# Moving two layers' seam: layer 2's first scores before layer 1's last down products, and a root taken on GpSimd

## The chip, the cores and the metric

The kernel runs on one core of a Trainium2 chip. A core has TensorE for matrix products (PE in the profile, its weight loads PEld), VectorE (DVE), ScalarE (ACT), GpSimd (POOL) and SyncE (SP), which here only starts transfers. Each engine works through its own queue of instructions in order, and waits at the head of the queue on semaphores of the others. The metric is the time of one execution on the device, in microseconds; lower is better.

## The reference

The whole is a stack of four layers over x of shape (4, 256, 256), that is 1024 tokens of width 256. Each layer adds a gated attention and a gated feed-forward, each over a layer norm of x:

```
x = x + tanh(g_xattn[n]) * attention_n(layernorm(x), ctx)
x = x + tanh(g_ffn[n])   * ffn_n(layernorm(x))

def layernorm(x):  (x - mean) / sqrt(var + 1e-5)

# layer 1's ffn: ternary weights
h = gelu(x @ w1_q.T + b1)            # 256 -> 1024
out = h @ w2_q.T + b2                # 1024 -> 256

# layer 2's attention: 16 heads of 16, 64 keys
scores = (q @ Wq.T) . k / 4, causal
out = softmax(scores) . v @ Wout.T

# layer 2's ffn: whole numbers of 8 bits
y = round(x / x_scale) @ round(w / w_scale).T * x_scale * w_scale + bias
```

The change lies at the seam between layer 1's feed-forward and layer 2's attention.

## The kernel before

The 1024 tokens are 8 tiles of 128 (t = 0 to 7), each held in SBUF as x[t]; four tiles make a group of 512 (g = 0, 1). The program is written as a list of steps (attention and feed-forward of the four layers). The order on each engine's queue is settled when the program is built, by a scheduler that takes instructions by their dependencies and by the order in which the code names them. `behind(later, sooner)` adds an order without a wait; `side_by_side` raises the priority of products that belong together. Tiles come from pools with a fixed number of buffers: four banks of PSUM under the tag mm, two double banks under wide, so a product may also wait until an older result has been copied out.

**Layer 1's feed-forward** (`ffn1`). `up(g)` makes the hidden values of a group in three bf16 terms, `down(g, i, terms)` multiplies them with the ternary w2 for one tile: 24 matmuls in one PSUM bank (L1920), then y = product + bias (L1928) and x[t] = gate * y + x[t] (`gated_add`, L517). The hidden values lie in the upper part of the large buffer `big`, where layer 3's last experts are to be loaded, so `load_experts3(EARLY3, E3)` and the load that follows `used("L1_w2")` wait for the last products.

Around the last four down products, `ffn1` already prepares layer 2: `keys_values` makes the keys and the values in steps (L1000, L1007, L1016, L171 and L169), `layernorm(0)` normalises group 0, `transposed` turns it (L461, copies L169 and L171), `head_queries` multiplies it with Wq (L476) and scales it in ScalarE (L1034). In the code the order is: down 0, normalise, down 1, down 2, down 3, transpose, queries.

**`layernorm`** (L425 to L452): for each tile the statistics (L430, L433) on VectorE; then for the group's four variances at once, in a tile of 128x4, the square root of var + eps on ScalarE (L435) and its reciprocal on VectorE (L438); then x - mean times that, tile by tile, on VectorE (L449), or, for layers where `scalar` is set, on ScalarE (L446) with a shift made on VectorE (L442).

**Layer 2's attention** (`attention23`). `scores(t)` makes one tile's scores: for even t a causal mask is put in first (L1065), then four products (L1075), the maximum over the keys (L1090), the difference in two halves (L1092) on VectorE, the exponential (L1101) on ScalarE. `weights` sums (L490), takes the reciprocal (L491) on VectorE and multiplies on GpSimd (L492). `attend(t)` transposes the weights (L506), copies them in ScalarE (L507), multiplies with the values (L1109), copies (L1118) and multiplies with Wout (L1121); `gated_add` (L517) then adds to x[t]. `in_flight` names these in stages: scores of tile i, the addition of tile i-3, the weights of tile i-1, the attend of tile i-2. In each of its rounds it takes one step of a generator `beside`: here `queries(1)`, which normalises, turns and multiplies group 1, together with the keys and values for layer 3 and, near the end, `rounded(0)`, the first part of layer 2's feed-forward.

[...] The profile shows a load (ACT_TABLE_LOAD, 1.28 us) where the queue goes from the gelu to the root, from the root to the exponential, and back to the root for layer 2's feed-forward.

Of the kernel before, what the change touches and what calls it, by code (L numbers as in the profile page):

```python
# [30 lines left out]
F32 = mybir.dt.float32  # L31
# [66 lines left out]
def tile_flamingo(ctx: ExitStack, tc: tile.TileContext, a: dict, out: bass.AP):  # L98
# [39 lines left out]
    def small(shape, name, bufs=3, dtype=F32):  # L138
        return sb.tile(shape, dtype, tag=name, name=name, bufs=bufs)

    def behind(later, sooner):

        tc.add_manual_dep(
            later.ins,
            sooner.ins.name,
            mybir.DependencyInfo(mybir.DependencyClass.NoSync, mybir.DependencyReason.DATA),
            reason="not sooner",
        )

    def side_by_side(products):  # L150

        last = None
        for product in products:
            with tc.high_priority(AT_ONCE) if last else nullcontext():
                made = product()
            if last:
                behind(made, last)
            last = made
        return last
# [26 lines left out]
    nc.gpsimd.memset(ones, 1.0)  # L186
    eps = const.tile([P, 1], F32, tag="eps", name="eps")
    nc.gpsimd.memset(eps, EPS)
    root = small([P, 1], "root", 1)
    nc.scalar.activation(root, eps, AF.Sqrt)  # L190

# [119 lines left out]
    def used(name):  # L311

        del loaded[name]
        at[1] += 1
        issue()
# [106 lines left out]
            nc.sync.dma_start(out=tiled(sums, layer)[:, t, :], in_=x[t])  # L422


    def layernorm(g, scalar=False, after=()):  # L425

        mv = small([P, TPG, 2], "mv")
        for i in range(TPG):
            st = small([P, 6], "st")
            made = nc.vector.bn_stats(st, x[g * TPG + i])  # L430
            if after:
                behind(made, after[0])
            nc.vector.bn_aggr(mv[:, i, :], st)  # L433
        rstd = small([P, TPG], "rstd")
        made = nc.scalar.activation(rstd, mv[:, :, 1], AF.Sqrt, bias=eps)  # L435
        if after:
            behind(made, after[1])
        nc.vector.reciprocal(rstd, rstd)  # L438
        xn = []
        if scalar:  # L440
            shift = small([P, TPG], "shift")
            nc.vector.scalar_tensor_tensor(shift, mv[:, :, 0], -1.0, rstd, ALU.mult, ALU.mult)  # L442
        for i in range(TPG):
            n = sb.tile([P, D], F32, tag="xn", name="xn", bufs=AHEAD + 2)
            if scalar:
                nc.scalar.activation(n, x[g * TPG + i], AF.Identity, bias=shift[:, i : i + 1], scale=rstd[:, i : i + 1])  # L446
                xn.append(n)
                continue
            kept["normal"] = nc.vector.tensor_scalar(  # L449
                n, x[g * TPG + i], mv[:, i, 0:1], rstd[:, i : i + 1], ALU.subtract, ALU.mult  # L450
            )
            xn.append(n)  # L452
        return xn
# [65 lines left out]
    def in_flight(scores, attend, gate, beside=iter(())):  # L519

        made, outs = {}, {}
        for i in range(NT + 3):
            next(beside, None)
            if i < NT:
                made[i] = scores(i)
            if i >= 3:
                gated_add(i - 3, outs.pop(i - 3)[:, :D], gate)
            if 1 <= i <= NT:
                weights(made[i - 1])
            if 2 <= i < NT + 2:  # L530
                outs[i - 2] = attend(i - 2, made.pop(i - 2))
# [505 lines left out]
    def attention23(layer, gate, beside):  # L1037
        kbd, vbd = kept.pop(layer)
        w = loaded[f"L{layer}"]
        w_o = w[:, 512:1024].rearrange("p (c o) -> p c o", c=2)  # L1040
        qT = []

        def queries(g):

            xn = layernorm(g, layer == 3)
            yield
            xT = transposed(xn)
            yield
            qT.append(head_queries(layer, xT))

        if (layer, 0) in kept:
            qT.append(kept.pop((layer, 0)))
        else:
            for _ in queries(0):
                pass

        def scores(t):


            g, i = divmod(t, TPG)  # L1060
            ps = ps_wide()
            masked = t % 2 == 0
            if masked:
                for a in range(2):
                    nc.tensor.matmul(  # L1065
                        ps[:, a, :].rearrange("p (h l) -> p h l", l=L),
                        ident16,
                        causal16.unsqueeze(1).to_broadcast([P, 8, L]),
                        start=True,
                        stop=False,  # L1070
                    )

            def part(half, a):
                rows = slice(a * L, (a + 1) * L)
                return nc.tensor.matmul(  # L1075
                    ps[:, a, half * D : (half + 1) * D],
                    qT[g][rows, half, i * P : (i + 1) * P],
                    kbd[rows, half, t // 2].rearrange("p i l -> p (i l)"),
                    start=not masked,
                    stop=(half == 1 or not masked),  # L1080
                )

            last = side_by_side(lambda half=half, a=a: part(half, a) for half in range(2) for a in range(2))
            if layer == 3 and t == 2:
                kept_busy(1, ps_mm(), last)

            e = t4([P, NH, L], "attn")
            src = ps.rearrange("p a (h l) -> p (a h) l", l=L)
            mx = small([P, NH], "mx")
            nc.vector.tensor_reduce(mx, src, AX.X, ALU.max)  # L1090
            for a in range(2):
                nc.vector.tensor_tensor(  # L1092
                    e.rearrange("p (f a i) l -> p a f i l", f=2, a=2)[:, a],
                    ps[:, a, :].rearrange("p (f i l) -> p f i l", f=2, l=L),
                    mx[:, a * 8 : (a + 1) * 8]
                    .rearrange("p (f i) -> p f i", f=2)
                    .unsqueeze(3)
                    .to_broadcast([P, 2, 4, L]),
                    ALU.subtract,
                )  # L1100
            nc.scalar.activation(e, e, AF.Exp)  # L1101
            return e

        def attend(t, e):
            aT = transposed_pairs(e)
            ps = ps_mm()
            for pr in range(NP):
                half, r = divmod(pr, 4)
                nc.tensor.matmul(  # L1109
                    ps[r * 32 : (r + 1) * 32, half * P : (half + 1) * P],  # L1110
                    vbd[:, t // 2, pr].rearrange("p j d -> p (j d)"),
                    aT[:, pr, :],
                    start=True,
                    stop=True,
                    tile_position=(0, r * 32),
                )
            cT = sb.tile([P, 2 * P], F32, tag="xn", name="ctxTok", bufs=AHEAD + 2)
            nc.scalar.copy(cT, ps[:, : 2 * P])  # L1118
            ps = ps_mm()
            for half in range(2):  # L1120
                nc.tensor.matmul(  # L1121
                    ps[:, :D], cT[:, half * P : (half + 1) * P], w_o[:, half, :], start=(half == 0), stop=(half == 1)
                )
            return ps

        in_flight(scores, attend, gate, zip_longest(queries(1), beside))
        if layer == 3:
            used("L3")

# [756 lines left out]
    def ffn1(gate):  # L1886
# [26 lines left out]
                three_terms([hidden[:, g, k, 2 * f2 : 2 * f2 + 2, :] for k in range(3)], h, h, f2 % 2 == 1)  # L1913
            return hidden[:, g]

        def down(g, i, terms):
            ps = ps_mm()
            for f in range(8):
                for k in range(3):
                    nc.tensor.matmul(  # L1920
                        ps[:, :D],
                        terms[:, k, f, i * P : (i + 1) * P],
                        w2[:, f, :],
                        start=(f == 0 and k == 0),
                        stop=(f == 7 and k == 2),
                    )
            y = sb.tile([P, D], F32, tag="xn", name="y", bufs=AHEAD + 2)
            nc.vector.tensor_tensor(y, ps[:, :D], b2_1, ALU.add)  # L1928
            gated_add(g * TPG + i, y, gate)

        terms = [up(g) for g in range(NG)]
        used("L1_w1")
# [3 lines left out]
        keys = keys_values(2, region("weff", 2048, "kbd2"), values[:, :1024])  # L1936
        next(keys)
        down(1, 0, terms[1])
        next(keys)
        xn = layernorm(0)  # L1940
        down(1, 1, terms[1])
        next(keys)
        down(1, 2, terms[1])
        for _ in range(2):
            next(keys)
        down(1, 3, terms[1])
        xT_2 = transposed(xn)
        for _ in keys:
            pass
        kept[2, 0] = head_queries(2, xT_2)  # L1950
        used("L1_w2")
        load_experts3(EARLY3, E3)


    def quantised():
# [252 lines left out]
```

## Time and profile before

| | |
|---|---|
| median of three runs | 826.48 us (822.49 to 829.31) |
| the profiled execution, its own time | 826.97 us |
| its span, first to last instruction | 825.1 us |
| granted TensorE clock, mean | 0.991 |
| TensorE, VectorE, ScalarE, GpSimd busy | 94%, 60%, 35%, 30% |
| layer 1's down products (L1920) | 509.73 to 533.5 us |
| layer 2's scores and attends (L1075 to L1121) | 538.97 to 588.4 us |
| layer 2's feed-forward starts on TensorE (L2025) | 588.20 us |
| first use of the load that waits for L1_w2 | 653.2 us |
| first expert of layer 3 on TensorE (L1451) | 703.2 us |

Times in the rows are microseconds from the start of the span. A line of the timeline gives the start, the time that the piece took, the engine, the line of the program, the operation, result and operands, the number of instructions, and in brackets the idle time before it and what ended that. A line of the windows gives the stretch, its length, the busy time of TensorE, its weight loads, VectorE, ScalarE and GpSimd (with the number of instructions), the granted clock, and the share and rate of the transfers. Where two lines overlap by some hundredths, the next instruction has started while the one before still drains.

### The profile page before, as it was taken

To read this page: it belongs to the slowest core of one execution; us is meant where nothing else is said; L and a number is where in the kernel's file an instruction comes from. 1 tells how busy PE (TensorE), PEld (TensorE's weight loads), DVE (VectorE), ACT (ScalarE), POOL (GpSimd) and SP (SyncE) were. 2 spreads that over 40 slices of the span, in tenths; PEclk is the share of its full clock that TensorE was granted. 3 is DMA by queue.
4 is the path that set the end of the run, shared out by engine and by line. 5 is a ranking of instruction groups with operands and counts; after the bars stand their busy time and mean duration, and the time that the engine had idled before them with its cause. 6 is when DMAs were issued, how large, how long until landed. Compare 5 with 4: busy or idle time off the path is not lost. (4 is left out here: it accounts for less than half of the span.)

```text
span 825.1 us, 12510 instructions
## 1 busy us (share of the span) xinstructions
PE 779.1 (94%) x4509; PEld 523.8 (63%) x4512; DVE 496.2 (60%) x1146; ACT 291.5 (35%) x508; POOL 245.9 (30%) x211
## 2 busy tenths in 40 slices
PE   6999999899999899999999999998898899999994
PEld 4544433777565677766656565755445656999993
DVE  4664455775594455543868759889779564334331
ACT  2221111443421333331643468266455421233320
POOL 0454544232113244322021110024424103444332
PEclk9999999999999999999999999999999999999998
DMA  9510114710021253333840001540000102232211
GB/s 340 198 39 1 39 58 160 274 38 26 26 67 48 63 125 68 73 78 77 296 156 1 8 1 33 191 166 1 26 1 2 52 9 78 53 49 44 29 16 18
DMA packets 32467, 62.44 MB, mean 76 GB/s; under 512 B 5552, under 2 KB 19504, under 8 KB 31696
## 3 DMA queue, kind: packets, MB, share of 16 engines
q1 hardware_dynamic: 25008, 51.91, 18.4%
q0 software_dynamic: 7104, 9.41, 6.8%
q8 instruction: 39, 0.64, 0.3%
q10 hardware_dynamic: 288, 0.26, 0.1%
q14 instruction: 28, 0.23, 0.1%
HBM read 52.81 MB, written 9.27 MB: 75 GB/s over the span
## 5 line engine op out<-in xcount | busy, mean ns | idle before, releaser
L492 POOL TENSOR_TENSOR attn<-attn,sm 128x1024 f32<-128x1024 f32 x32 | 61.1, 1911 | 217.9 <-DVE sm L491 169.1
L476 PE MATMUL wide<-xT,big 128*128 128x512 f32 (+1 forms) x240 | 108.7, 600 | 1.1 <-DVE shared L1678 0.9
L742 DVE TENSOR_TENSOR rope<-wide,big 128x512 f32<-128x512 f32 x96 | 59.6, 682 | 52.1 <-PE wide L476 52.1
L476 PEld LDWEIGHTS wide<-xT,big 128*128 128x128 f32 (+1 forms) x240 | 43.7, 189 | 57.3 <-issue 49.2
L1451 PE MATMUL wide<-blk,still 128*128 128x128 f32 x640 | 74.8, 275 | 0.6 <-DVE blk L1423 0.6
L1451 PEld LDWEIGHTS wide<-blk,still 128*128 128x128 f32 x640 | 73.1, 192 | 0.8 <-issue 0.8
L714 PE MATMUL mm<-vo,attnT 128*128 128x256 f32 x256 | 58.6, 382 | 1.5 <-ACT attnT L507 1.5
L476 PE MATMUL wide<-xT,dense 128*128 128x512 f32 (+1 forms) x120 | 55.1, 599 | 0.0
L714 PEld LDWEIGHTS mm<-vo,attnT 128*128 128x128 f32 x256 | 47.8, 190 | 11.4 <-ACT attnT L507 3.3
L507 ACT COPY attnT<-mm 128x512 f32<-128x512 f32 x64 | 34.6, 587 | 45.6 <-PE mm L506 45.1
L490 DVE TENSOR_REDUCE sm<-attn 128x16 f32<-128x1024 f32 x32 | 38.7, 1208 | 15.2 <-ACT attn L484 13.8
L1413 DVE COPY still<-big 128x1024 f32 x20 | 13.9, 693 | 52.1 <-PE wide L1451 44.7
L1485 POOL DMA_INDIRECT out_dram<-ring,scratch x20 | 31.5, 1577 | 39.3 <-DVE ring L1478 15.7
L1485 POOL DMA_INDIRECT sums<-ring,big x17 | 26.9, 1584 | 48.4 <-ACT ring L1567 18.8
L506 PE MATMUL mm<-ident,attn 128*128 128x128 f32 x256 | 35.4, 284 | 4.5 <-POOL attn L492 4.5
L1469 PE MATMUL mm<-big,hidden 128*128 x160 | 37.8, 380 | 1.4 <-DVE hidden L1462 1.4
L1386 POOL DMA_INDIRECT xs<-xd,scratch x20 | 20.0, 999 | 63.2 <-PE mm L1420 36.7
L506 PEld LDWEIGHTS mm<-ident,attn 128*128 128x128 f32 x256 | 30.6, 146 | 12.6 <-POOL attn L492 7.7
L1461 ACT ACTIVATE hidden<-wide 128x512 f32<-128x512 f32 x20 | 11.9, 597 | 71.2 <-PE wide L1451 66.1
L476 PEld LDWEIGHTS wide<-xT,dense 128*128 128x128 f32 (+1 forms) x120 | 21.5, 185 | 24.4 <-issue 22.0
L517 DVE SCALAR_TENSOR_TENSOR x<-mm,tg,x 128x256 f32<-128x256 f32 x44 | 20.4, 469 | 26.9 <-PE mm L714 15.0
L750 POOL TENSOR_TENSOR rotated<-rope 128x512 f32<-128x512 f32 x12 | 15.3, 1271 | 58.6 <-DVE rope L742 58.6
(363 smaller groups left out, 1572.2 us busy)
## 6 DMA issues: line engine op xcount, KB each, us to landing
big<-in_L_w_gate_up SPq DMA_DIRECT2D x8, 1024.0 KB, 10.4
big<-in_L_w_down SPq DMA_DIRECT2D x8, 512.0 KB, 11.0
w_L_qk<-in_L_qk SPq DMA_DIRECT2D x4, 896.0 KB, 9.5
big<-in_L_w SPq DMA_DIRECT2D x2, 1480.0 KB, 8.1
big<-in_L_w SPq DMA_DIRECT2D x2, 1110.0 KB, 5.2
big<-in_L_wo SPq DMA_DIRECT2D x1, 2048.0 KB, 15.0
big<-in_L_w SPq DMA_DIRECT2D x2, 1024.0 KB, 5.4
xd<-xn SPq DMA_DIRECT2D x16, 128.0 KB, 1.8
```

What stands on the lines that cost most here:

```text
L476: nc.tensor.matmul(ps, w(c), xT[:, c, :], start=(c == 0), stop=(c == 1))
L490: nc.vector.tensor_reduce(sm, e, AX.X, ALU.add)
L492: nc.gpsimd.tensor_tensor(e, e, sm.unsqueeze(2).to_broadcast([P, groups, n]), ALU.mult)
L506: nc.tensor.transpose(ps[:, i * P : (i + 1) * P], ev[:, pr * P : (pr + 1) * P], ident)
L507: nc.scalar.copy(aT[:, half * 4 : half * 4 + 4, :].rearrange("p i t -> p (i t)"), ps)
L517: return nc.vector.scalar_tensor_tensor(x[t], ps, gate, x[t], ALU.mult, ALU.add)
L714: nc.tensor.matmul(ps[:, :D], aT[:, s, :], vo[:, s, :], start=(s == 0), stop=(s == NP - 1))
L742: nc.vector.tensor_tensor(m[:, s, :].rearrange("q (b t) -> q b t", t=S), ps[:, s, :].rearrange("q (b t) -> q b t", t=S), table, ALU.mult,)
L1386: nc.gpsimd.indirect_dma_start(out=xs, out_offset=None, in_=self.xd, in_offset=bass.IndirectOffsetOnAxis(ap=self.gather[:, b : b + 1].bitc ...
L1451: made = nc.tensor.matmul(ps[:, k, f : f + P], w[:, at : at + P], st[:, c * P : (c + 1) * P], start=(c == 0), stop=(c == 1),)
L1469: made = nc.tensor.matmul(ps[:, :D], hT[:, j * P : (j + 1) * P], self.w[:, bass.ds(r + j * D, D)], start=(j == 0), stop=(j == n - 1),)
L1485: nc.gpsimd.indirect_dma_start(out=self.sums[b % len(self.sums)], out_offset=bass.IndirectOffsetOnAxis(ap=self.scatter[:, b : b + 1].bitca ...
```

## The change

Three things are changed.

1. `layernorm` gets a second way to take the root, used for layer 2's attention in the group that is normalised there (group 1): VectorE adds eps to the four variances, and GpSimd raises the sum to the power -0.5 with a constant tile. ScalarE's root and VectorE's reciprocal are left out there. All other layer norms are as before.
2. In `ffn1`, group 0 is normalised and turned before and beside the second down product of group 1, and its queries are made before the third. The third and fourth down products are put into a generator, `down_2`, which is kept and run as the first of the steps beside layer 2's attention, ahead of `queries(1)`.
3. Each of these two down products is bound behind the scores last made (`kept["scored"]`), so that the first follows tile 0's scores and the second tile 1's. The release of w2 and the loads of the last experts go with them.

```diff
+    power = const.tile([P, 1], F32, tag="power", name="power")
+    nc.gpsimd.memset(power, -0.5)
...
-    def layernorm(g, scalar=False, after=()):
+    def layernorm(g, scalar=False, after=(), powered=False):
...
-        made = nc.scalar.activation(rstd, mv[:, :, 1], AF.Sqrt, bias=eps)
-        if after:
-            behind(made, after[1])
-        nc.vector.reciprocal(rstd, rstd)
+        if powered:
+            nc.vector.tensor_scalar_add(rstd, mv[:, :, 1], EPS)
+            nc.gpsimd.tensor_tensor(rstd, rstd, power.to_broadcast([P, TPG]), ALU.pow)
+        else:
+            made = nc.scalar.activation(rstd, mv[:, :, 1], AF.Sqrt, bias=eps)
+            if after:
+                behind(made, after[1])
+            nc.vector.reciprocal(rstd, rstd)
...
-            xn = layernorm(g, layer == 3)
+            xn = layernorm(g, layer == 3, powered=(layer == 2))
...
-            last = side_by_side(lambda half=half, a=a: part(half, a) for half in range(2) for a in range(2))
+            kept["scored"] = last = side_by_side(lambda half=half, a=a: part(half, a) for half in range(2) for a in range(2))
...
-        in_flight(scores, attend, gate, zip_longest(queries(1), beside))
+        in_flight(scores, attend, gate, zip_longest(chain(kept.pop("others", ()), queries(1)), beside))
...
-        def down(g, i, terms):
+        def down(g, i, terms, after=None):
...
+                    if after is not None:
+                        behind(made, after)
...
+        def down_2():
+            yield
+            down(1, 2, terms[1], kept["scored"])
+            yield
+            down(1, 3, terms[1], kept["scored"])
+            used("L1_w2")
+            load_experts3(EARLY3, E3)
...
         down(1, 0, terms[1])
+        xn = layernorm(0)
         next(keys)
-        xn = layernorm(0)
         down(1, 1, terms[1])
-        next(keys)
-        down(1, 2, terms[1])
+        xT_2 = transposed(xn)
         for _ in range(2):
             next(keys)
-        down(1, 3, terms[1])
-        xT_2 = transposed(xn)
+        kept[2, 0] = head_queries(2, xT_2)
         for _ in keys:
             pass
-        kept[2, 0] = head_queries(2, xT_2)
-        used("L1_w2")
-        load_experts3(EARLY3, E3)
+        kept["others"] = down_2()
```

As the scheduler then orders the queues: TensorE runs the second down product, group 0's transposes, one product of the keys and one of the values, the queries of group 0, three products of the values, tile 0's scores, the third down product, tile 1's scores, the fourth down product, tile 2's scores, tile 0's transposes (L506), tile 3's scores, the rest of tile 0's attend, group 1's transposes, tile 1's attend, group 1's queries, tile 4's scores, and then tile 2's transposes. Before, group 1's transposes and queries lay around tile 1's scores, and tile 4's scores in the middle of tile 0's attend. On GpSimd the power stands between the products (L492) of tile 0 and tile 1. From layer 2's feed-forward on, every engine's order is as before.

More of the change, by code (lines that the diff above doesn't have):

```diff
@@ L1919, in down @@
                 for k in range(3):
-                    nc.tensor.matmul(
+                    made = nc.tensor.matmul(
                         ps[:, :D],
```

## The prediction, as put on record

> **What bounds the kernel now.** I read the page first, then 5 us windows over the stage that the change touches, then the timelines of TensorE, VectorE and GpSimd there. (The chain that ended last names only the closing output writes, so it says nothing here.)
>
> ```profile
> span 825.1 us, 12510 instructions
> PE 779.1 (94%) x4509; PEld 523.8 (63%) x4512; DVE 496.2 (60%) x1146; ACT 291.5 (35%) x508; POOL 245.9 (30%) x211
> ```
>
> TensorE is busy 94% of the span, but that mixes stages. The windows (PE, PEld, DVE, ACT, POOL busy, granted clock, DMA) part them:
>
> ```profile
> 525.00:530.00 5.00, 5.00 (x41) 3.86 (x39) 4.74 (x15) 0.00 (x0) 0.00 (x0) 1.00 0.79 299
> ...
> 555.00:560.00 5.00, 4.51 (x39) 2.83 (x38) 5.00 (x9) 3.43 (x7) 2.21 (x2) 1.00 0.00 0
> ...
> 575.00:580.00 5.00, 3.41 (x27) 2.17 (x26) 3.54 (x7) 2.45 (x5) 1.90 (x1) 0.81 0.00 0
> 580.00:585.00 5.00, 4.19 (x36) 3.22 (x35) 2.01 (x6) 3.27 (x7) 1.15 (x2) 0.84 0.00 0
> ```
>
> In the down products TensorE is the limit (5.00 of 5). In the middle of layer 2's attention VectorE is (5.00 of 5). From 575 on neither is: there it is a chain through transposes, ScalarE copies and products, one tile after another, and part of it runs at a lower clock. TensorE's timeline shows that chain:
>
> ```profile
> 560.74 1.09 PE L506 MATMUL mm<-ident,attn 128*128 128x128 f32 x8
> ...
> 574.58 1.04 PE L506 MATMUL mm<-ident,attn 128*128 128x128 f32 x8
> 576.65 0.91 PE L1109 MATMUL mm<-attnT,values 128*32 128x128 f32 x16 [1.03 <-ACT attnT L507]
> 578.06 2.02 PE L1121 MATMUL mm<-w_L,ctxTok 128*128 128x256 f32 x4 [0.49 <-ACT ctxTok L1118]
> 579.87 1.86 PE L506 MATMUL mm<-ident,attn 128*128 128x128 f32 x8
> ...
> 584.30 1.04 PE L506 MATMUL mm<-ident,attn 128*128 128x128 f32 x8
> ```
>
> L506 begins the attend of a tile: tile 2 at 560.74, tile 5 at 574.58, 6 at 579.87, 7 at 584.30. L1121 takes 2.02 and L506 1.86 where others take 1.13 and 1.04. VectorE:
>
> ```profile
> 540.48 1.22 DVE L1090 TENSOR_REDUCE mx<-wide 128x16 f32<-128x1024 f32 x1 [2.27 <-PE wide L1075]
> ...
> 555.85 1.21 DVE L1090 TENSOR_REDUCE mx<-wide 128x16 f32<-128x1024 f32 x1
> ...
> 576.65 1.80 DVE L442 SCALAR_TENSOR_TENSOR shift<-mv,rstd 128x4 f32<-128x4 f32 x1
> ...
> 598.64 0.16 DVE L442 SCALAR_TENSOR_TENSOR shift<-mv,rstd 128x4 f32<-128x4 f32 x1
> ```
>
> Tile 0's maximum starts at 540.48 after 2.27 us of waiting, tile 4's at 555.85. The last two lines are one instruction on the same shape: 0.16 us alone, 1.80 us beside this one on GpSimd, which ended at 578.43:
>
> ```profile
> 576.53 1.90 POOL L492 TENSOR_TENSOR attn<-attn,sm 128x1024 f32<-128x1024 f32 x1 [3.47 <-DVE rstd L438]
> ```
>
> So a VectorE instruction that reads two operands from SBUF stands still while GpSimd runs L492. L1863, a tensor_scalar, shows the same: 0.47 us at 455.75, 1.73 us at 451.97, beside the L492 of 451.20 to 453.42. L449, also a tensor_scalar, took 1.62 us for four at 461.67 instead of 1.37 at 525.38, its first beside an L492 that ended at 462.18. L442 and L1863 ended 0.0 to 0.3 us after L492. Instructions that read PSUM (L1090, L1092) and the statistics (L430) keep their length beside L492.
>
> **The change, part by part.**
>
> *Early scores, the gain.* Both kernels agree until 526.27, the end of the second down product of group 1. After it TensorE now has 8 transposes (0.96), one key product (0.63), one value product (0.53), the query product of group 0 (3.63), three value products (1.60) and tile 0's scores (1.07), by the rows of L461, L1000, L1016, L476, L1075: scores end at 534.69. VectorE's own work (y, kbd, values) ends near 534.3, so tile 0's maximum starts at 534.75, 5.7 us earlier than 540.48. The third down product (2.69, from 24 matmuls of L1920) ends at 537.38, tile 1's scores at 539.08, the fourth at 541.77, tile 2's at 544.00. TensorE's work is only reordered; the gain is that 5.4 us of down products cover the softmax.
>
> *What pays for it.* Group 1's normalisation (needs the fourth down product), transposes and queries (0.96 + 3.63) move from 536–546 into the attention loop. On TensorE's queue tile 4's scores stand behind tile 1's attend and these queries. That is the new critical chain, which I follow by row lengths:
> VectorE: maximum 0 to 535.93, subtraction (L1092 x2, 1.20) to 537.12; the down's y, x and statistics to 538.9; maximum 1 from 539.13, sum 0 (1.13), subtraction 1, reciprocal 0 at 542.60. GpSimd's L492 of tile 0 starts 0.42 after it (as 547.34 to 547.76 before). Then y, x, statistics of the fourth down, sum 1, maximum 2, the added 128x4 add at 546.8, half of subtraction 2, and the xn (L449 x4, 1.29) from 547.6 if nothing blocks. xn 548.9, second half 549.5, maximum 3, x of tile 0, xT copy to 551.7, subtraction 3 to 552.9. ScalarE's exponential of tile 3 (1.05) now stands ahead of tile 1's ctxTok copy (0.37): 554.4. TensorE: tile 1's output product 554.5 to 555.55, queries to 559.2, value product to 559.8, tile 4's scores end 560.8. Maximum 4 at 560.85: already 5.0 later than before, while VectorE idles some 4 us. Tile 3's sum has been done meanwhile.
>
> *From tile 4 to the end of the stage.* TensorE then starts tile 2's attend at about the same 560.8 as before (560.74). Before, 560.74 to tile 7's L506 took 23.56. Of this 2.30 was excess: the same tail in layer 3 runs at 3.71 a tile (640.80, 644.51, 648.22), against 5.29 and 4.43 here, from the table load for the root (574.53, 1.28) ahead of tile 5's copies (the 1.03 wait) and the clock. In the new ScalarE order that load stands behind tile 5's copies, so I take the excess away. Tile 5's scores (1.07) are still to be done, one value product (0.63) fewer: 21.7. Tile 7's L506 at 582.5, 1.8 earlier.
>
> *GpSimd in the way, two stalls.* First, the x of the fourth down (L517 with y and x, both SBUF) is issued 0.61 after reciprocal 0, L492 of tile 0 at 0.42. It stands until about L492's end: 1.5 us late; sum 1 had 0.3 of slack, so 1.2. Second, the power releases xn, but L492 of tile 1 is next on GpSimd's queue and its reciprocal is ready, so it starts the moment the power ends, before VectorE hears of it. The add at m, the power from m+0.32 to m+0.32+P, L492 to m+2.22+P, xn from 0.25 before that, against m+0.95: 1.0 + P late. Together 2.2 + P, all on the chain above. If VectorE always came first it would be 0.
>
> *The power itself, P.* No row shows it. From below 0.09 us (the smallest GpSimd row, L188 128x1); from above 1.91 (L492, the longest arithmetic row). The rows nearest in size are 0.29 (L492 on 128x64); a power should cost several products, so P = 0.5. Stalls: 2.7. [...]
>
> *The clock.* Before, TensorE was busy 0.62, 0.35 and 0.50 in the three microseconds from 575, and from 578.2 to 581.4 the clock was half: 0.89 + 0.82 = 1.7 us. In the new order TensorE has, between 549.2 and tile 1's output product (some 557), only 3.7 us of work, less than half busy. I expect the half clock there, ahead of that product and the queries, which are on the chain: 1.7. Bounds 0 and 1.7. [...]
>
> *At nothing.* The sqrt (0.30) and reciprocal (0.18) of group 1 go, one 128x4 add (0.17) comes: within 0.2. No table load is added, since the power takes the root off ScalarE. The memset of the constant (0.09) lies in GpSimd's idle 18.35 us before 19.82. SP's last loads (shared_gate_up, two gate_up, one w_down, issued 533.5 to 535.6) wait for the last two down products and go 8 us later; nothing else stands on SP until 588.4, they land in 7 to 11 us, and first use is at 653.2 and 703.2. With that cover gone they would cost at most those 8 us. From layer 2's feed-forward on the order on every queue is unchanged, so the shift is carried to the end.
>
> *Sum.* -1.8 + 2.7 + 1.7 = +2.6 us. The profiled execution took 826.97 (825.1 of span, 1.9 around it), so 829.6; it lay 0.5 above the median 826.48, so the median goes to 829.1.
>
> **Rivals.**
> *Not slower: VectorE gets the ports first.* If L517 or xn starts before L492, GpSimd waits instead (L492 took 2.22 at 451.20, where 1.90 is usual), and the stalls fall to about 0.3; TensorE's gap is then too short for the clock. -1.8 + 0.3 = -1.5: 825.0. It decides if both stalls together stay under 1.8 and the clock holds. Against it: L492 leads by 0.19 and by a semaphore's time.
> *A dear power.* P of 3 to 6 us makes the same chain 2.5 to 5.5 longer: 831.6 to 834.6. For it: no row of any such function on GpSimd. Against: 128x4 is tiny.
> *Given back, no difference.* The stalls are there but the clock holds, or the excess of the tail returns: -1.8 + 2.7 = +0.9: 827.4. [...]
>
> **How the numbers follow.** Forecast 0.45, ports first 0.20, dear power 0.15, given back 0.20. The forecast's own range is 827.5 to 831 (P from 0.1 to 1.9, the clock in part). The three runs lie 822.49 to 829.31, so a median carries 1 to 2 us. For 8 in 10: from 824 (the first rival less 1) to 833.5 (most of the dear power). 1%, 8.3 us, is about what a measurement of this kernel can tell from no change. Faster by that needs all waits of the stage gone: 0.02. Slower by that needs P over 6: 0.07. Same: 0.91. The predicted time is the forecast's, 829.1.
>
> **What would show it.** Early scores right: tile 0's L1090 near 534.8. The chain: tile 4's L1090 after a VectorE idle of 4 us or more on PE wide, at 563 to 566; if it starts before 558 the chain is wrong. Stalls: the last L517 on y at 1.5 to 2 us instead of 0.48, and the first xn of group 1 behind GpSimd's second L492. P is read off its own row. Clock: granted 0.5 near 553 to 561, none near 578. Tail: L506 of tiles 5 to 7 spaced 3.7. End: tile 7's L506 2 to 3 after 584.30. I am wrong if the power takes over 2 us, or if ScalarE's order in the tail still puts the load ahead of copies.

## The result, and the profile after

The changed kernel takes 829.93 us in the median of 20 executions (825.67 to 832.93), the kernel before 825.3 us in the median of 20 (822.32 to 829.31). The ratio is 1.0057, with a 95% interval of 1.0041 to 1.0073: slower by 3.4 to 6.0 us, which is within the 1%, 8.3 us, that the prediction counts as no change. The forecast was 829.1 us (824.0 to 833.5).

In the changed kernel the line numbers are higher by 2 to 12 (in the kernels of the experiments by a few more): L438 is now the added add, L439 the power, L455 makes xn (L449 before), L467 transposes (L461), L482 is the query product (L476), L496 and L497 are the softmax's sum and reciprocal on VectorE and L498 its product on GpSimd (L490 to L492), L512 opens an attend (L506), L523 adds to x (L517), L1096 is the maximum (L1090), L1127 the output product (L1121). The first lines of its page:

```profile
span 827.6 us, 12513 instructions
...
PE 778.6 (94%) x4509; PEld 524.2 (63%) x4512; DVE 497.8 (60%) x1146; ACT 291.8 (35%) x507; POOL 246.9 (30%) x213
```

The profiled execution took 829.47 us. TensorE does the same work, and the span is 2.5 us longer. The 5 us windows of the stage (PE, PEld, DVE, ACT, POOL busy, granted clock, DMA):

```profile
550.00:555.00 5.00, 4.10 (x14) 2.75 (x15) 5.00 (x10) 2.05 (x4) 0.61 (x1) 0.60 0.74 285
555.00:560.00 5.00, 4.50 (x30) 2.78 (x29) 3.79 (x7) 2.50 (x4) 1.90 (x1) 0.71 0.01 3
560.00:565.00 5.00, 5.00 (x23) 2.64 (x22) 1.23 (x6) 1.71 (x4) 1.90 (x1) 1.00 0.00 0
...
575.00:580.00 5.00, 4.15 (x34) 2.55 (x33) 4.03 (x6) 3.83 (x7) 1.91 (x1) 1.00 0.00 0
580.00:585.00 5.00, 3.86 (x41) 2.69 (x41) 4.01 (x16) 3.71 (x7) 3.77 (x2) 1.00 0.00 0
```

Two things have changed places. The low clock, 0.81 and 0.84 at 575 to 585 before, is now at 550 to 560 (0.60 and 0.71), and the tail runs at full clock. And VectorE, 5.00 of 5 in the middle of the stage before, is idle for most of 560 to 565 (1.23 of 5) while TensorE is full. TensorE's timeline shows why:

```profile
550.90 2.21 PE L467 MATMUL mm<-ident,xn 128*128 128x128 f32 x8 [2.04 <-DVE xn L455]
...
554.19 1.97 PE L512 MATMUL mm<-ident,attn 128*128 128x128 f32 x8
...
558.51 1.13 PE L1127 MATMUL mm<-w_L,ctxTok 128*128 128x256 f32 x4 [0.50 <-ACT ctxTok L1124]
559.48 3.60 PE L482 MATMUL mm<-xT,w_L 128*128 128x512 f32 x8
...
576.17 1.09 PE L512 MATMUL mm<-ident,attn 128*128 128x128 f32 x8
579.93 1.04 PE L512 MATMUL mm<-ident,attn 128*128 128x128 f32 x8
583.63 1.04 PE L512 MATMUL mm<-ident,attn 128*128 128x128 f32 x8
587.33 1.04 PE L512 MATMUL mm<-ident,attn 128*128 128x128 f32 x8
```

TensorE stands empty for 2.04 us until group 1's xn are there, then works at half clock (0.50 in the windows of 1 us from 552 to 557; 2.21 us for group 1's eight transposes, where the same row behind a wait for xn takes 1.64 to 1.65 in the profiles below in which the clock held over it, and 1.97 us for tile 1's, where others take 1.04 to 1.09), and reaches the queries only at 559.48. The last four lines are the attends of tiles 4 to 7, 3.70 to 3.76 apart. Tile 7's starts 3.03 us later than before. VectorE:

```profile
534.46 1.22 DVE L1096 TENSOR_REDUCE mx<-wide 128x16 f32<-128x1024 f32 x1 [0.29 <-PE wide L1081]
...
542.70 2.04 DVE L523 SCALAR_TENSOR_TENSOR x<-y,tg,x 128x256 f32<-128x256 f32 x1
...
548.76 2.96 DVE L455 TENSOR_SCALAR xn<-x,mv,rstd 128x256 f32<-128x256 f32 x4 [0.47 <-POOL rstd L439]
...
564.62 1.23 DVE L1096 TENSOR_REDUCE mx<-wide 128x16 f32<-128x1024 f32 x1 [3.73 <-PE wide L1081]
```

Tile 0's maximum starts 6.0 us earlier, tile 4's 8.8 us later. Between them stand the fourth down product's x (2.04 us instead of 0.48) and group 1's four xn (2.96 instead of 1.38). In the kernel before the two rows are:

```profile
533.97 0.48 DVE L517 SCALAR_TENSOR_TENSOR x<-y,tg,x 128x256 f32<-128x256 f32 x1
...
536.82 1.38 DVE L449 TENSOR_SCALAR xn<-x,mv,rstd 128x256 f32<-128x256 f32 x4
```

In the changed kernel GpSimd is at work beside both:

```profile
542.56 1.90 POOL L498 TENSOR_TENSOR attn<-attn,sm 128x1024 f32<-128x1024 f32 x1 [62.04 <-DVE sm L497]
...
547.67 1.05 POOL L439 TENSOR_TENSOR rstd<-rstd,power 128x4 f32<-128x4 f32 x1 [3.21 <-DVE rstd L438]
548.71 1.90 POOL L498 TENSOR_TENSOR attn<-attn,sm 128x1024 f32<-128x1024 f32 x1
```

The power takes 1.05 us, and tile 1's L498 starts the moment it ends, 0.05 us ahead of xn.

### The profile page after: what moved, and what is told of

It reads as the page before. It is cut to its first block, busy times and chain, and to the rows that moved or that the text cites. A ratio compares the mean times of both kernels' runs of the same rounds, so it can differ in the third digit from the quotient of the medians.

```text
span 827.6 us, 12513 instructions
## 1 busy us (share of the span) xinstructions
PE 778.6 (94%) x4509; PEld 524.2 (63%) x4512; DVE 497.8 (60%) x1146; ACT 291.8 (35%) x507; POOL 246.9 (30%) x213
## 5 line engine op out<-in xcount | busy, mean ns | idle before, releaser
L498 POOL TENSOR_TENSOR attn<-attn,sm 128x1024 f32<-128x1024 f32 x32 | 61.1, 1911 | 222.5 <-DVE sm L497 177.8
L482 PE MATMUL wide<-xT,big 128*128 128x512 f32 (+1 forms) x240 | 108.8, 601 | 1.1 <-DVE shared L1684 0.9
L482 PEld LDWEIGHTS wide<-xT,big 128*128 128x128 f32 (+1 forms) x240 | 43.7, 189 | 57.4 <-issue 49.5
L482 PE MATMUL wide<-xT,dense 128*128 128x512 f32 (+1 forms) x120 | 55.1, 599 | 0.0
L496 DVE TENSOR_REDUCE sm<-attn 128x16 f32<-128x1024 f32 x32 | 38.7, 1208 | 14.5 <-ACT attn L490 13.8
L512 PE MATMUL mm<-ident,attn 128*128 128x128 f32 x256 | 35.4, 284 | 4.5 <-POOL attn L498 4.5
L512 PEld LDWEIGHTS mm<-ident,attn 128*128 128x128 f32 x256 | 30.5, 146 | 12.8 <-POOL attn L498 7.4
L523 DVE SCALAR_TENSOR_TENSOR x<-mm,tg,x 128x256 f32<-128x256 f32 x44 | 20.4, 470 | 27.9 <-PE mm L720 15.0
L482 PEld LDWEIGHTS wide<-xT,dense 128*128 128x128 f32 (+1 forms) x120 | 21.5, 185 | 24.4 <-issue 22.0
```

What stands on the lines that cost most here:

```text
L482: nc.tensor.matmul(ps, w(c), xT[:, c, :], start=(c == 0), stop=(c == 1))
L496: nc.vector.tensor_reduce(sm, e, AX.X, ALU.add)
L498: nc.gpsimd.tensor_tensor(e, e, sm.unsqueeze(2).to_broadcast([P, groups, n]), ALU.mult)
L512: nc.tensor.transpose(ps[:, i * P : (i + 1) * P], ev[:, pr * P : (pr + 1) * P], ident)
L523: return nc.vector.scalar_tensor_tensor(x[t], ps, gate, x[t], ALU.mult, ALU.add)
```

## The experiments

A ratio below is known to some 1.3 to 2.5 us each way. The traces are finer. I read one length from each: from the start of the x of group 1's second down product, the last that all kernels have in the same place (L517 at 527.35 before, L523 at 527.49 in the changed kernel), to the start of tile 7's attend (584.30 and 587.33). This is called the stage. "TensorE time lost" is, over the stage's windows, busy time times one minus the granted clock.

| run | median, us | ratio to before (95%) | stage, us | lost to the clock in the stage, us |
|---|---|---|---|---|
| the kernel before | 825.3 | 1 | 56.95 | 1.7 |
| the changed kernel | 829.93 | 1.0057 (1.0041 to 1.0073) | 59.84 | 3.4 |
| the same again | 829.40 | 1.0054 (1.0031 to 1.0077) | 61.81 | 4.7 |
| power alone | 823.91 | 1.0004 (0.9983 to 1.0025) | 56.86 | 1.7 |
| reorder alone, root on ScalarE | 829.00 | 1.0059 (1.0040 to 1.0078) | 60.89 | 1.7 |
| first stall taken away | 825.14 | 1.0007 (0.9987 to 1.0028) | 57.10 | 0 |
| second stall taken away | 825.04 | 0.9993 (0.9970 to 1.0015) | 56.79 | 0 |
| both taken away | 824.81 | 1.0002 (0.9983 to 1.0020) | 55.51 | 0 |
| both taken away, again | 824.16 | 1.0003 (0.9983 to 1.0023) | 55.51 | 0 |
| reorder alone, both taken away | 826.54 | 1.0006 (0.9987 to 1.0026) | 57.28 | 0 |
| queries ahead of tile 1's attend | 830.15 | 1.0058 (1.0037 to 1.0080) | 60.24 | 3.4 |
| unused products in the empty stretch | 825.94 | 1.0013 (0.9989 to 1.0037) | 61.89 | 4.7 |
| the same again | 828.21 | 1.0057 (1.0030 to 1.0085) | 58.37 | 0 |
| power twice | 856.05 | 1.0397 (1.0366 to 1.0427) | 60.70 | 3.2 |

The runs were made in three sets, each on one chip with its own runs of the kernel before (medians 824.36, 827.28 and 824.23 us), to which the ratio is taken. The ratio is the record's and not the quotient of two medians: the times of the kernel before lie mostly in two groups, near 823.5 and 827.5, and its median falls now in one, now in the other. So ratios are to be compared, not medians of different sets.

In six of the seven profiles in which both stalls are left after the reorder, the clock fell in this stage ahead of or during group 1's queries; in the five with one stall or both taken away it held through the whole stage.

**The power alone**, in the kernel before:

```diff
-            xn = layernorm(g, layer == 3)
+            xn = layernorm(g, layer == 3, powered=(layer == 2))
```

> The kernel before with only the root of layer 2's second group moved to GpSimd as a power; the down products stay where they were. My theory (what costs is where the power meets GpSimd's softmax products, not the power): here the root falls at about 536, 11 us before GpSimd's first L492, so it meets nothing. The power takes 1.05 us as in after's row, xn starts about 1.2 us later (538.0 instead of 536.8), and its transposes do not start before 540.36 in any case: the kernel before within 0.5 us, 824.8 to 825.8 beside 825.3. Rival, the power itself is what makes the changed kernel slow: 1 to 3 us above the kernel before.

As my theory had it: 1.0004, and the stage is 56.86 against 56.95. Its GpSimd and its VectorE:

```profile
533.86 1.05 POOL L439 TENSOR_TENSOR rstd<-rstd,power 128x4 f32<-128x4 f32 x1 [56.17 <-PE mm L482]
```

```profile
534.95 1.38 DVE L455 TENSOR_SCALAR xn<-x,mv,rstd 128x256 f32<-128x256 f32 x4 [1.17 <-POOL rstd L439]
```

The same 1.05 us, but with no L498 near it the four xn take 1.38, and their transposes stand behind tile 0's scores on TensorE, where they start 1.36 us after the last xn. The power by itself costs nothing there.

**The reorder alone**, in the changed kernel:

```diff
-            xn = layernorm(g, layer == 3, powered=(layer == 2))
+            xn = layernorm(g, layer == 3, powered=False)
```

> The changed kernel with the root of the second group back on ScalarE, so only the reorder of the down products is left. My theory (the chain through group 1's normalisation, transposes and queries eats the early gain, and GpSimd's L498 stalls VectorE beside it): the stalls stay, because both L498 stay where they are; P of 1.05 us goes, but ScalarE loads its table twice more (1.28 us each) between exponentials. 1 below to 1 above the changed kernel, so 3 to 5 us above the kernel before. Rival, only the power is to blame: the early start shows as a gain, 1 to 2 us below the kernel before.

As my theory had it: 1.0059, as slow as the changed kernel. The x of the fourth down takes 2.04 us again, xn 2.01, and the clock falls later, over the queries (4.82 us instead of 3.60).

**Both stalls taken away.** `apart` adds a wait on a semaphore; tile 0's L498 is held until the fourth down's x is made, tile 1's until the last xn. `hold` is set ahead of layer 2's attention, so it meets tile 0:

```diff
-        nc.gpsimd.tensor_tensor(e, e, sm.unsqueeze(2).to_broadcast([P, groups, n]), ALU.mult)
+        def scaled():
+            return nc.gpsimd.tensor_tensor(e, e, sm.unsqueeze(2).to_broadcast([P, groups, n]), ALU.mult)
+        if kept.pop("hold", None):
+            kept["scaled"] = scaled
+        else:
+            made = scaled()
+            if kept.pop("turn", None):
+                apart(made, kept["normal"])
...
-            gated_add(g * TPG + i, y, gate)
+            added = gated_add(g * TPG + i, y, gate)
+            if "scaled" in kept:
+                apart(kept.pop("scaled")(), added)
+                kept["turn"] = True
```

> The changed kernel with two waits added on GpSimd: tile 0's L498 starts after the x of the fourth down product, tile 1's L498 after the last xn of group 1, so neither VectorE row runs beside an L498. My theory: x takes 0.48 instead of 2.04 us and xn 1.4 instead of 2.96; the transposes come 2.5 to 3 us earlier, TensorE's empty stretch at 549 to 551 shrinks with it and the half clock goes or shortens; tile 1's L498 ends some 0.5 us later than in the changed kernel and is not the last to be waited for. 2 to 4 us below the changed kernel, 0.5 to 2.5 above the kernel before; tile 4's maximum at 561 to 562.5 instead of 564.62. Rival, the stalls lie beside the path: the same as the changed kernel within 0.7 us.

```profile
543.86 0.48 DVE L532 SCALAR_TENSOR_TENSOR x<-y,tg,x 128x256 f32<-128x256 f32 x1
...
548.65 1.38 DVE L455 TENSOR_SCALAR xn<-x,mv,rstd 128x256 f32<-128x256 f32 x4 [0.47 <-POOL rstd L439]
```

Both rows are at their plain length, TensorE has no wait over 0.9 us from 545 on, and the clock stays at 1.00 through the stage. The stage is 4.33 us shorter than the changed kernel's, tile 4's maximum comes 25.83 us after tile 0's instead of 30.16, and the time is that of the kernel before. The drop below the changed kernel, 4.5 us by the two ratios, is a little larger than the 2 to 4 expected.

**One stall at a time**, with one of the two waits each:

> The changed kernel with the first stall alone taken away: tile 0's L498 on GpSimd starts after the x of the fourth down product; tile 1's L498 is left beside xn. My theory: x takes 0.48 instead of 2.04 us, the group's chain comes 1.2 us earlier, the xn still take 2.96 and TensorE's empty stretch stays 2 us long, so the half clock stays: 1.2 us below the changed kernel (0.6 to 2). If the clock holds, 3 or more below. Rival, the two stalls cost only by way of the clock: then this one alone is worth nothing or everything (0, or 4 us).

> The changed kernel with the second stall alone taken away: tile 1's L498 on GpSimd starts after the last xn of group 1; tile 0's L498 is left beside the fourth down product's x. My theory: the four xn take 1.4 instead of 2.96 us, TensorE restarts 1.6 us earlier after an empty stretch of 0.5 instead of 2.04 us, and the half clock of 6.5 us goes with it: 3 to 4 us below the changed kernel. Rival, the stalls count by their length alone: 1.6 below.

Without the first stall xn starts 13.03 us after tile 0's maximum instead of 14.30, without the second the four xn take 1.38 instead of 2.96: 1.27 and 1.58 us. The clock held in both. That was expected for the second, and not for the first: there TensorE's wait for xn shrank from 2.04 to 0.46 us because xn comes 1.3 us earlier and tile 0's output product ends 0.3 us later, which I had not worked out. From the end of the last xn to the start of the queries it is 6.29 us in these two and with both stalls gone, and 7.76 in the changed kernel.

**The queries ahead of tile 1's attend**: `queries` does not stop between the transposes and the query product.

```diff
             xT = transposed(xn)
-            yield
+            if layer == 3:
+                yield
             qT.append(head_queries(layer, xT))
```

> The changed kernel with group 1's queries issued one turn earlier, so that on TensorE they stand ahead of tile 1's attend. My theory (tile 4's scores wait for the queries behind tile 1's attend): the queries start when the xT copies are done, near 554.5 instead of 559.48; tile 4's maximum at 560 to 562 at the full clock, at 563 if the half clock falls on the queries. 1 to 4 us below the changed kernel. Rival, the end of the stage is set by TensorE's total work and not by tile 4's scores: the same as the changed kernel within 0.7 us, since tile 1's attend is only moved behind.

```profile
551.46 4.02 PE L482 MATMUL mm<-xT,w_L 128*128 128x512 f32 x8
...
556.04 1.10 PE L512 MATMUL mm<-ident,attn 128*128 128x128 f32 x8
...
573.01 1.97 PE L512 MATMUL mm<-ident,attn 128*128 128x128 f32 x8
```

My theory fell here; by the time, the rival was right. Tile 4's maximum comes 3.9 us earlier (26.26 after tile 0's), and the time is the changed kernel's. Tile 1's attend, the second line, now comes 24.06 us after tile 0's maximum instead of 19.73, and the attends of tiles 2 to 4 come only 0.6, 1.2 and 0.7 us earlier. TensorE is full, or nearly, in either order from the queries to tile 3's attend; tile 4's scores are one of several things that wait for it. But the two profiles are not at the same clock. Here it fell twice, over the transposes and the start of the queries and again from 572.6 to 576.0, over tile 4's attend (the third line); tile 5's attend is then 0.4 us later than in the changed kernel, counted from tile 0's maximum. So what the earlier scores are worth at an even clock stays open.

**Something for TensorE in the empty stretch**: three products that nothing uses, behind tile 0's output product.

```diff
+            if layer == 2 and t == 0:
+                idle = ps_mm()
+                for _ in range(3):
+                    made = nc.tensor.matmul(
+                        idle.rearrange("p (h l) -> p h l", l=L),
+                        ident16,
+                        causal16.unsqueeze(1).to_broadcast([P, 8, L]),
+                        start=True,
+                        stop=True,
+                    )
+                    behind(made, last)
+                    last = made
```

> The changed kernel with three bf16 products of 128x512 that nothing uses (0.30 us each) on TensorE behind tile 0's output product, in the stretch at 549 to 551 where it waits for xn; both stalls stay. The planner then puts half of tile 3's subtraction ahead of VectorE's xT copy, 0.6 us that the queries do not wait for. My theory (the clock falls because of this stretch, and its 6.5 us at half speed are on the path): the clock holds and 1.7 to 3 us go, 827 to 828.3. Rivals: the clock falls all the same, since what remains of the stretch is 1.1 us (no change); or the clock holds and the time stays, because the work at half clock lay beside waits (no change, clock at 1.0).

> The changed kernel with the three unused products in TensorE's empty stretch once more. Its first profile showed the clock fall there all the same, for some 10 us, and a stage of 54.9; its 12 times lay in two groups, 5 at 829.9 to 831.6 and 7 at 824.3 to 826.1. My theory: the groups are executions in which the clock fell in this stage and in which it held. Either the clock is at half there again and the stage takes 54 to 55, with a time near 830; or it holds and the stage takes 51.4, since the stalls are still there, with a time 3 to 4 lower. Rival, the groups come from elsewhere in the program: a time near 825 with the clock at half in this stage.

With them TensorE waits 1.39 us for xn. In the first profile the clock fell all the same, in the second it held, so the products do not settle the clock; the two ratios, 1.0013 and 1.0057, leave it as open. The times of the two profiled executions, 830.25 and 824.89 us, differ by 5.4 us, of which 3.5 lie in the stage, so the groups of times come from this stage and from elsewhere too. But the second profile shows what was asked: both stalls, no low clock anywhere in the program while TensorE works, and a stage of 58.37 us; from tile 0's maximum 51.40, where 51.4 was worked out.

```profile
548.10 1.64 PE L467 MATMUL mm<-ident,xn 128*128 128x128 f32 x8 [1.39 <-DVE xn L455]
...
551.19 1.06 PE L512 MATMUL mm<-ident,attn 128*128 128x128 f32 x8 [0.82 <-DVE x L523]
...
555.21 3.60 PE L482 MATMUL mm<-xT,w_L 128*128 128x512 f32 x8
```

So the stalls alone are 58.37 - 55.51 = 2.86 us, and the low clock of the changed kernel's profile 59.84 - 58.37 = 1.47 us. The runs with one stall each bear this out, at an even clock too: the stage is 57.10 - 55.51 = 1.59 us longer with the second stall alone, 56.79 - 55.51 = 1.28 with the first alone, and 2.87 is their sum.

**The changed kernel again, and both stalls taken away again**, on one chip:

> The changed kernel once more, for a second profile and beside the other three on one chip. By the runs so far, the stage from tile 0's maximum to tile 7's transposes took 52.87 us in the changed kernel, 50.12 and 49.82 with one stall taken away, 48.53 with both. From the last xn's end to group 1's queries it took 7.76 with the half clock and 6.29 in each of the three runs without, so the half clock is 1.5 us of the path. My theory: TensorE's empty stretch at 14.5 to 16.5 after tile 0's maximum comes in every execution, so the clock falls there again: 52.9. If it holds this time: 51.4. Rival, the half clock is worth the whole difference: with the clock held, 48.5 to 49.

> Both stalls taken away once more, on the same chip as the changed kernel. My theory: the stage takes 48.5 us, no half clock at 549 to 558, and the time is 3.5 to 5 us below the changed kernel's of this call, within 1.5 of the kernel before. Rival, the first run's clock held by chance and the stalls are worth only 2.9 us (1.3 and 1.6): 2.9 below the changed kernel, with half clock in this stage in the profile.

The clock fell again, but later and for longer, from about 553.9 to 564.1: it caught tile 1's transposes and output product and a part of the queries.

```profile
559.75 2.07 PE L1127 MATMUL mm<-w_L,ctxTok 128*128 128x256 f32 x4 [0.49 <-ACT ctxTok L1124]
561.61 4.85 PE L482 MATMUL mm<-xT,w_L 128*128 128x512 f32 x8
```

In the first profile these were 1.13 and 3.60 us. The stage is 61.81 us, so the low clock cost 61.81 - 58.37 = 3.44 us this time; I had expected 1.5. Without the stalls the stage is the same 55.51 to a hundredth, and the median is 5.2 us below the changed kernel's (4.2 by the ratios).

**The power twice in a row**:

```diff
             nc.gpsimd.tensor_tensor(rstd, rstd, power.to_broadcast([P, TPG]), ALU.pow)
+            nc.gpsimd.tensor_tensor(rstd, rstd, power.to_broadcast([P, TPG]), ALU.pow)
```

> The changed kernel with the power made twice in a row on GpSimd, so that group 1 is scaled by another root than the reference's; nothing else is left out or moved. The rival of the prediction, a dear power, and my theory agree that the power is on the path while it stands between the added add and xn: the xn start and GpSimd's L498 of tile 1 come 1.05 us later, the stage takes 53.9 instead of 52.87, or 52.5 if the clock holds. If the power's time is covered (VectorE has the rest of tile 2's subtraction and the next maximum to do, but they stand behind xn): no change in the stage.

```profile
544.07 1.05 POOL L439 TENSOR_TENSOR rstd<-rstd,power 128x4 f32<-128x4 f32 x1 [3.21 <-DVE rstd L438]
545.20 1.02 POOL L440 TENSOR_TENSOR rstd<-rstd,power 128x4 f32<-128x4 f32 x1
```

The xn start 1.09 us later and the stage is 0.86 longer, with the low clock in both profiles: in the changed kernel, other than in the run with the power alone, its time is on the path nearly in full. The median of 856.05 says nothing of it: from tile 7's attend to the end it takes 268.9 us instead of 240.3, with TensorE busy for 35.6 us behind 800 instead of 15.8. The values are altered here, so what comes later may differ for that; I did not pursue it.

**The reorder alone, both stalls taken away**: the edits of the second and the third experiment together.

> The reorder of the down products alone, with both stalls taken away: the root of the second group is on ScalarE, and L498 of tiles 0 and 1 start after x and after the last xn. In the run with the root on ScalarE and the stalls left, xn started 2 us earlier than behind the power (14.36 after tile 0's maximum against 14.30 and 13.02 of them with the stall of x, by the two traces) and the tail was not shorter. My theory (the stalls pay for the time, the power only 1 us of it): the time of the run without the stalls and with the power within 1 us, so 823.5 to 825.5. Rival, the table loads on ScalarE (1.28 us each) take the power's place as the cost: 826 or more.

One sentence of that expectation is misread: 14.36 and 14.30 are the same, so xn had not started earlier with the root on ScalarE. By the medians it cannot be told from the run with the power (1.0006 and 1.0002). By the traces the root on ScalarE costs 57.28 - 55.51 = 1.77 us more than the power, the rival's way. ScalarE's timeline:

```profile
547.21 1.28 ACT L1116 ACT_TABLE_LOAD   x1
548.50 1.06 ACT L1116 ACTIVATE attn<-attn 128x1024 f32<-128x1024 f32 x1
549.46 0.35 ACT L1133 COPY ctxTok<-mm 128x256 f32<-128x256 f32 x1
```

The load back to the exponential stands ahead of tile 0's ctxTok copy, and TensorE's output product waits 1.47 us for that copy, with group 1's transposes behind it. In this order of the downs, then, the power on GpSimd is the better root; the L498 behind it makes that hard to see.

No version beats the kernel before by more than can be measured. The two runs without stalls come out even with it.

## Why the prediction was right, and where it was not

**The early start.** Predicted 534.75 for tile 0's maximum, measured 534.46. The gain that is left with stalls and low clock gone is 56.95 - 55.51 = 1.44 us; 1.8 was predicted. The tail is as predicted: spaced 3.7, no low clock, the table load behind tile 5's copies. The kernel before has its 1.7 us of low clock in this tail in both of the profiles that keep its order, so the gain is that loss avoided: 56.95 less the 1.71 us that two rows there lost (2.02 and 1.86 us instead of 1.13 and 1.04) would be 55.24, no longer than the 55.51. By this estimate, which no run shows, the reorder brings nothing at an even clock, and the head start of 6 us is used up before tile 7.

**The stalls.** Predicted 2.7, measured 2.86. The first was 1.2 and is 1.27. The second was 1.0 + P with P = 0.5, and is 1.58 for the xn beside L498. The power itself was the mis-sized term: 1.05 us and not 0.5. Counted as the prediction did, from an xn that starts 0.95 after the add, the second stall is 1.58 and 0.38 (xn starts 1.33 after the add), 1.96 in all, where its formula gives 2.05 with the measured P. The 0.38 is in the run without stalls too, so here it lessens the 1.44 rather than raising the 2.86; by the prediction's own counting the gain is 1.82 and the stalls are 3.23.

**The low clock, the step that failed.** Predicted 1.7, with bounds 0 and 1.7, on tile 1's output product and the queries. It cost 1.47 in the first profile, but on the transposes and tile 1's transposed weights; 3.44 in the second, on the product and the queries as predicted; and nothing in the profile with the unused products where it held. The upper bound was wrong: I took the one fall seen in the kernel before, 3.4 us long, as the most there could be, and the low clock lasted 6.8 us in the first profile and 10.2 in the second. For the first profile the parts are -1.44 + 2.86 + 1.47 = +2.89 us. They add up by construction, being differences of the same four stages; the check on them is the span, which is 2.5 us longer.

**The chain.** That the wait ahead of tile 4's maximum shows the delay was right (564.62, predicted 563 to 566, VectorE idle 3.73 us before it, predicted 4 or more). That tile 4's scores set the end was not shown: moved 3.9 us ahead they left the time as it was, in a profile with a second stretch of low clock behind them.

**At nothing.** The loads that go later are all but over at 555 (DMA share 0.01 in the 5 us behind it), and from tile 7's attend to the end it takes 240.3 us in the first profile and 240.8 in the second, 240.8 before: nothing was lost there. The power alone makes 1.0004, at most 1.0025 or 2.1 us.

**The rivals.** "Ports first" did not happen: L498 led both times, by 0.14 us and by 0.05 (no row shows ports; what the rows show is which started first). "Dear power" neither, 1.05 us. "Given back" is what the second profile with the unused products shows: +1.42 in the stage, predicted +0.9.

**The median.** That 829.1 is so near to 829.93 is luck: the base of three runs, 826.48, was 1.2 above the median of 20, and the difference of the medians is 4.6, not 2.6. The second profile's difference in the stage is 4.86 (its execution, 833.43 us, is the slowest of its twelve), the first's 2.89, so low clock that varies from one execution to the next is the likely cause of the rest. The record has the granted clock of the executions: its mean is 0.9886 over 32 of the changed kernel and 0.9911 over 97 of the kernel before. That is 2.1 us of clock in 825, and not all of it need cost time; the mean times are 829.50 and 825.28, 4.2 apart. So about half of the difference can be the clock, and the other half is near the 1.42 that the stage shows for the stalls less the gain. What each execution lost where was not counted.

## What to carry to other kernels

When work of one engine moves, look up in the timeline what will run beside it on an engine that can hold it up: here two stalls of 1.3 and 1.6 us, and the low clock that came with them, cost more than a head start of 6 us had brought, and holding GpSimd back for as long made the loss good. A head start is worth only what the busiest engine can use of it: ask when TensorE next stands empty, and for how long, before counting the microseconds at the front. And price a clock fall as something that may come or not, at more than one length: here, in this stage, it took 0, 1.7, 3.2 to 3.4 or 4.7 us of TensorE's work.

## What the runs showed of the hardware

**The low clock came in stretches of 3.4, 6.8 or 10.2 us, and not in the same place each time.** That is up to 800 us, where the windows of 1 us show a stretch whole: the clock in it was 0.50, and it lasted 3.38 to 3.42 us most often, 6.82 in the changed kernel's first profile and 10.24 in its second. Where it fell once, TensorE lost 1.47 to 1.71 us of work, most often 1.70 or 1.71; in the changed kernel's first profile 3.41, and in its second 4.7, with some waits of TensorE in the stretch. Elsewhere in the program it fell at 270 and 461 in one execution of the kernel without stalls, and at 597 (four matmuls of L527 took 3.51 us, where fourteen had taken 6.17) and 658 in the next. TensorE's wait before the fall was 1.03 us in the kernel before, 2.04 in the changed one and 1.39 beside the unused products (where it once fell and once held), and the clock held after a wait of 1.47 us in the reorder with both stalls taken away and of 0.46 with one. So the length of one wait does not decide it; what does was not settled.

**Two VectorE rows ended with GpSimd's L498 beside them.** The x took 2.04 instead of 0.48 us in all eight profiles in which tile 0's L498 was left beside it; in the changed kernel it ended 0.28 us after L498. That is an instruction with two operands in SBUF; the tensor_scalar that makes xn did the same (the first of the four took 2.00 us, where four take 1.38 without L498, and ended 0.15 after it). Why they wait was not shown.

**A power on GpSimd took 1.05 us for 128x4** in ten profiles, and 1.02 as the second of two in a row; the product on 128x64 took 0.29 in the kernel before.
